# A two-layer graph network on one core: another buffer for the first score row, another place for half of the first mask's loads, and two copies and two comparisons of the last part moved to VectorE

## The chip, the cores and the metric

The kernel runs on one core of a Trainium2 chip. The metric is the device time of one execution in microseconds (us); before the change the median of three runs is 2143.52 us (2142.39 to 2146.54). The core has a matrix engine (TensorE, PE in the profile), VectorE (DVE), ScalarE (ACT), GpSimd (POOL) and SyncE (SP). SP and POOL issue DMA transfers here, each in the order of its own instruction stream.

## The reference, cut to what matters

```python
# 3327 nodes, 1024 features, adj 3327 x 3327 (about 1 % non-zero)
# layer 0
h = maximum(layernorm(x), 0);  x = x + quantised(adj @ quantised(relu(quantised(h) @ quantised(weight))))
# layer 1: 8 heads of 64
h = maximum(layernorm(x), 0)
Wh = einsum('nf,hfd->hnd', h, W)
e_src, e_dst = (Wh * a1).sum(-1), (Wh * a2).sum(-1)
e = where(adj > 0, leaky_relu(e_src[:, :, None] + e_dst[:, None, :], 0.2), -9e15)
h = elu(einsum('hnm,hmd->hnd', softmax(e), Wh))
enc = h.transpose(1, 0, 2).reshape(n, 512)
out = relu(enc @ W1.T + b1); out = relu(out @ W2.T + b2); out = relu(out @ W3.T + b3)
x = x + out @ W4.T + b4
```

## The kernel before, in words

Nodes are padded to 26 tiles of 128. The work has four stages, one after the other on TensorE.

**Stage 1** (to about 127 us) forms the quantised product of the first layer, `s_int`, one tile of 128 nodes at a time.

**Stage 2** (the loop at L709, to about 922 us) multiplies the adjacency by `s_int`. For each output tile t, column t of the adjacency comes from memory in four pieces (`PARTS`, L48: source tiles 0-6, 7-12, 13-19, 20-25), each into an `at` buffer (L186). ScalarE rounds it to `hi` (L190), VectorE forms `lo = at - hi` (L194), and TensorE multiplies both with `s_int` (L723). VectorE also writes a mask of non-zeros, which POOL stores to memory (`mask_d`, L201). Then ScalarE empties the sum into `y` (L738), VectorE adds x, which POOL stores (L741), and normalises it (L149). `transposed_by_dma` (L607) has ScalarE split `y` into 16-bit halves (`yh`, L616, two casts) and SP issue two transposing DMAs (`yht`, L618); ScalarE joins the halves again to `ht` (L622, two copies). `heads` (L645) multiplies `ht` by the weights of all heads (`whm`, L652, 16 passes), forms the scores of source and destination, their exponentials (`powers`: L672 and two at L692) and the features of the tile, which POOL stores (`feat_d`, L703). The product `whm` of tile t stands on TensorE ahead of the last piece of tile t+1. For tiles 24 and 25 there is no such cover: TensorE runs the adjacency product of tile 25, then `whm` of tile 24, then attention work in between. Tile 25 is transposed on TensorE itself in two groups of four (`tp`, L638) with one shared PSUM buffer; ScalarE copies each group out (L642).

**Stage 3**, attention (the loop at L954), is a list of 32 parts: 8 heads times 4 subsets of the output tiles (`SUBS`, 7, 6, 7 and 6 tiles). A part goes through 13 pairs of source tiles in seven groups (`GROUPS`, L49: pairs 0-1, 2-3, 4-5, 6, 7-8, 9-10, 11-12). `select` makes the 0/1 choice of a pair: `over` says where the score is positive, by two ScalarE instructions (L845) or, for the pairs in `BY_VECTOR`, two VectorE instructions (L839); two VectorE instructions combine it with the mask to `sel` (L854, L855). `over` has two buffers, `sel` six. `sums` multiplies `sel` with the features (`acc`, L874). `select` runs two groups ahead of `sums`. The score row of a part (`srow`, one row of `src_d` copied to all partitions, L809) has two pools with one buffer each, `srow1` for odd parts and `srow0` for even ones; a pool that is opened earlier gets the lower address. These pools lie in space that `at`, `hi` and `lo` used in stage 2, so their first use waits for the last reader of what lay there.

At the turn from stage 2 to stage 3 the order on each engine is set by `queue_behind` (an instruction stands behind another on its queue) and `tc.issue_after`. L930-L944 issue the first loads: the mask of part 0 in two halves (source tiles 0-12 and 13-25, seven transfers each) on POOL; on SP the first score row, the two transposing DMAs of tile 24 behind it (L932), the x rows of tile 25, the features of head 0 in three pieces (tiles 0-6, 7-19, 20-23), the second score row, then the other masks. `pin` keeps the order of stage 3 on each engine as written.

**Stage 4** is a network of four dense layers over groups of four tiles. Its first two layers for the first group are woven into the last part of stage 3: `join` (L1024) makes 32-bit features from two 16-bit halves by four ScalarE copies (k = 0 to 3), and `layer` (L1029) is a generator that yields after each matmul, with one PSUM buffer and a ScalarE relu after k = 3 (L1043). In the last part the loop takes (0, 0, 3, 3, 2, 2, 2) steps of it ahead of the sums of groups 0 to 6 (L1069-L1073), so that k = 3 of the first output block and k = 0, 1 of the second stand between groups 2 and 3. ScalarE's stream there holds, in order: the four copies of `join`, the four `over` of pairs 7 and 8, the cast `eh` (L920) of the previous part's result, the four `over` of pairs 9 and 10, the relu.

Of the kernel before, what the change touches and what calls it, by code (L numbers as in the profile page):

```python
# [24 lines left out]
T = (N + P - 1) // P  # L25
NP = T * P
TH = T // 2
# [39 lines left out]
def two_layer_kernel(  # L67
# [23 lines left out]
    nc = tc.nc  # L91
# [62 lines left out]
    def queue_behind(ins, other):  # L154

        tc.add_manual_dep(
            ins.ins,
            other.ins.name,
            mybir.DependencyInfo(mybir.DependencyClass.NoSync, mybir.DependencyReason.DATA),
            reason="queue_behind",  # L160
        )

    def halves_of_words(words):

        return words.bitcast(U16).rearrange("p (n two) -> p two n", two=2)
# [7 lines left out]
    with tc.tile_pool(name="at", bufs=2, reuse_waits="tile") as atp:  # L173
# [42 lines left out]
        with tc.tile_pool(name="s1", bufs=2, reuse_waits="tile") as s1, tc.tile_pool(  # L216
            name="s1_mm", bufs=3, space=PSUM, reuse_waits="tile"
# [8 lines left out]
            def pin(ins):  # L226
                tc.keep_in_program_order(ins)
# [336 lines left out]
            for t in range(8, T):  # L564
                if t == T - 2:
                    part = next(columns)
                pair = t // 2 + 2
# [25 lines left out]
        with tc.tile_pool(name="wh", bufs=1, reuse_waits="tile") as whp, tc.tile_pool(  # L593
            name="s2", bufs=2, reuse_waits="tile"
        ) as s2, tc.tile_pool(name="mm", bufs=2, space=PSUM, reuse_waits="tile") as mm_ps, tc.tile_pool(
            name="s2_wh", bufs=2, space=PSUM, reuse_waits="tile"
        ) as wh_ps, tc.tile_pool(name="s2_sp", bufs=1, space=PSUM, reuse_waits="tile") as sp_ps, tc.tile_pool(
            name="s2_last", bufs=1, space=PSUM, reuse_waits="tile"
# [32 lines left out]
            def transposed_by_tensor(y):  # L631

                ht = s2.tile([P, KF, P], F32, name="ht", bufs=1)
                ends, copies = [], []
                for g in range(KF // 4):
                    tp = last_ps.tile([P, 4, P], F32, tag="last", name="tp2")
                    turns = [
                        nc.tensor.transpose(tp[:, q, :], y[:, (4 * g + q) * P : (4 * g + q + 1) * P], ident)  # L638
                        for q in range(4)
                    ]  # L640
                    ends.append((turns[0], turns[-1]))
                    copies.append(nc.scalar.copy(ht[:, 4 * g : 4 * g + 4, :], tp))  # L642
                return ht, ends, copies
# [65 lines left out]
            for t in range(T):  # L709
                xt = s2.tile([P, F], F32, name="xt2")  # L710
# [49 lines left out]
            of_k, products, _, powers, _, taken = heads(*before, own=f_even)  # L760
            queue_behind(products[0], lacking)
            queue_behind(taken, lacking)
            ht, turns, copies = transposed_by_tensor(y)
            queue_behind(copies[0], taken)
            queue_behind(powers[0], copies[-1])
            last_of_k, *_ = heads(T - 1, ht, r, own=f_even)

    attends = [(h, si) for h in range(NH) for si in range(len(SUBS))]
    steps = [(i, g) for i in range(len(attends)) for g in range(len(GROUPS))]
    AHEAD = 2  # L770
    BY_VECTOR = (6,)

    with tc.tile_pool(name="over", bufs=2, reuse_waits="tile") as overp, tc.tile_pool(
        name="srow1", bufs=1, reuse_waits="tile"
    ) as srow1, tc.tile_pool(name="srow0", bufs=1, reuse_waits="tile") as srow0, tc.tile_pool(
        name="sel", bufs=6, reuse_waits="tile"
    ) as selp, tc.tile_pool(name="f1", bufs=1, reuse_waits="tile") as f1p, tc.tile_pool(
        name="s3", bufs=1, reuse_waits="tile"
    ) as s3, tc.tile_pool(
        name="s3_acc", bufs=7, space=PSUM, reuse_waits="tile"  # L780
# [11 lines left out]
        def load_features(h, js):  # L792
            r = slice(js[0], js[-1] + 1)
            return nc.sync.dma_start(
                (f_odd if h % 2 else f_even)[:, r], feat_d[r, h].rearrange("t p c -> p t c")
            )

        def load_mask(si, js=slice(0, T), queue=nc.sync):
            for b, t in enumerate(SUBS[si]):
                ins = queue.dma_start(masks[si][:, b, js], mask_d[t][:, js])  # L800
            return ins
# [3 lines left out]
        def load_src(i):  # L805
            h, si = attends[i]
            nb = len(SUBS[si])
            srows[i] = (srow1 if i % 2 else srow0).tile([P, 7 * P], F32, tag="srow", name="srow")[:, : nb * P]
            return nc.sync.dma_start(srows[i], src_d[si][h].partition_broadcast(P))  # L809
# [17 lines left out]
        def select(n):  # L827
            ends = {}
            i, g = steps[n]
            h, si = attends[i]  # L830
            nb = len(SUBS[si])
            mask = masks[si].bitcast(U32)
            for pair in GROUPS[g]:
                over = overp.tile([P, 2, 7 * P], U8, tag="over", name="over")[:, :, : nb * P]
                for q in range(2):
                    j = 2 * pair + q
                    if pair in BY_VECTOR:
                        pin(
                            nc.vector.tensor_scalar(  # L839
                                over[:, q], srows[i], ndst[:, j, h : h + 1], 255.0, ALU.is_gt, ALU.mult  # L840
                            )
                        )
                    else:
                        ends["scalar"] = pin(
                            nc.scalar.activation(  # L845
                                over[:, q], srows[i], AF.Relu, bias=large_dst[:, j, h : h + 1], scale=BIG
                            )
                        )
                        ends.setdefault("first", ends["scalar"])
                sel = selp.tile([P, 2, 7, 2, P], U8, tag="sel", name="sel")  # L850
                up, dn = (sel[:, q, :nb].bitcast(U32) for q in range(2))
                of_pair = mask[:, :, 2 * pair : 2 * pair + 2]
                over = over.bitcast(U32).rearrange("p q (b i) -> p b q i", b=nb)
                pin(nc.vector.tensor_tensor(up, over, of_pair, ALU.bitwise_and))  # L854
                ends["vector"] = pin(nc.vector.tensor_tensor(dn, up, of_pair, ALU.bitwise_xor))  # L855
                chosen[i, pair] = sel.bitcast(F8)
            return ends
# [69 lines left out]
                )  # L927
            yield

        for js in (slice(0, TH), slice(TH, T)):  # L930
            load_mask(0, js, nc.gpsimd)
        queue_behind(planes[0], load_src(0))  # L932
        with tc.issue_after(turned.ins):
            ins = load_features(0, range(7))
        with tc.issue_after(ins.ins):
            load_features(0, range(7, 20))
            load_features(0, range(20, T - 2))
            load_src(1)
            load_mask(1)
            load_mask(2)  # L940
            ins = load_mask(3)
        with tc.issue_after(ins.ins):
            load_features(1, range(T - 2))
            load_features(1, range(T - 2, T))  # L944
        ends = select(0)
        queue_behind(joins[0], ends["scalar"])
        queue_behind(joins[1], joins[0])
        queue_behind(emptied, joins[1])
        queue_behind(resumed, ends["vector"])
        select(1)  # L950
        turn = [(of_k[-1], turns[0][0]), (turns[-1][1], last_of_k[0]), (last_of_k[-1], None)]
        closed = None
        first_group = iter(())
        for n, (i, g) in enumerate(steps):  # L954
            if n + AHEAD < len(steps):
                ends = select(n + AHEAD)
                if n == 0:
                    queue_behind(ends["first"], taken)
# [6 lines left out]
            if (i, g) == (len(attends) - 1, 0):  # L965
# [4 lines left out]
                def nodes(name):  # L970
                    n = large(mlp, name, [P, WORDS])
                    return (
                        n[:, : 4 * EMB].bitcast(U16).rearrange("p (q r) -> p q r", q=2),
                        n[:, 4 * EMB : 4 * (EMB + F)].rearrange("p (q e) -> p q e", q=4),
                    )

                weights = large(mlp, "weights", [P, WORDS])
                enc_x1 = [nodes("nodes0")]
# [5 lines left out]
                h1_0, h2_0, enct0 = (  # L984
                    rest[:, F + 16 + 512 * at : F + 16 + 512 * (at + n)].rearrange("p (m c) -> p m c", c=512)
                    for at, n in ((0, D1 // P), (D1 // P, D2 // P), ((D1 + D2) // P, EMB // P))
                )
# [8 lines left out]
                def by_feature(enc, cols):  # L996

                    k = EMB // P
                    return enc[:, :, : k * cols].rearrange("p q (k c) -> p q k c", k=k)
# [21 lines left out]
                nc.sync.dma_start(bb4, b4.partition_broadcast(P))  # L1021
                load_encoded(1, range(4, 8))

                def join(xt, enc):  # L1024

                    for k in range(EMB // P):
                        pin(nc.scalar.copy(halves_of_words(xt[:, k]), by_feature(enc, 512)[:, :, k]))  # L1027

                def layer(yt, xt, wt, bt):  # L1029
                    for m in range(yt.shape[1]):  # L1030
# [37 lines left out]
                first_group = early_layers()  # L1068
            if i == len(attends) - 1:  # L1069
                if g == 1:  # L1070
                    join(enct0, enc_x1[0][0])
                for _ in range((0, 0, 3, 3, 2, 2, 2)[g]):
                    next(first_group)  # L1073
            first, last = sums(n)
# [9 lines left out]
            if (i, g) == (len(attends) - 1, 5):  # L1084
                weight_sums()
                join(joined_1, enc_x1[1][0])
# [5 lines left out]
    with tc.tile_pool(name="s4", bufs=2, reuse_waits="tile") as s4, tc.tile_pool(  # L1092
        name="s4_ps", bufs=4, space=PSUM, reuse_waits="tile"
# [172 lines left out]
```

## Time and profile before

| what | value |
|---|---|
| median of three runs | 2143.52 us (2142.39 to 2146.54) |
| the profiled execution | 2143.69 us |
| its span, first to last instruction | 2141.8 us |
| mean granted TensorE clock | 0.996 |
| busy: PE, DVE, ACT, POOL | 2099.7 (98%), 1392.0 (65%), 1346.9 (63%), 163.6 us (8%) |
| the chain that ended last | PE 94%, DVE 2%, DMA 2%, ACT 2% |
| HBM read, written | 141.21 MB, 66.02 MB |

All instants in the text are us from the start of the span, so 1.9 us of the profiled time lie around it. Busy time says how long instructions of an engine were in work. The chain of waits is followed back from the last instruction to whatever released each one. A row of the timeline gives start, length, engine, line, operation, tiles and count, and in brackets the idle time before it with its releaser; SPq rows are issues of DMAs, not the transfers. A row of the stretches gives the busy time of each engine, the granted TensorE clock as a share of full speed, the share of the 16 DMA engines in work (it can pass 1) and GB/s.

### The profile page before, as it was taken

How to read it: one execution, taken by the hardware profiler on the slowest of the kernel's cores; microseconds unless marked ns; L12 is line 12 of the kernel's file. 1: busy time of each engine (PE TensorE's matmuls, PEld its weight loads, DVE VectorE, ACT ScalarE, POOL GpSimd, SP SyncE). 2: the span in 40 equal slices, each digit the busy share in tenths (PEclk: the TensorE clock that was granted, in tenths of full speed). 3: DMA queues.
4: the chain of work that ended last, by engine and by line, in shares of the span. 5: the costliest groups of instructions: out<-in, count | busy, mean ns of one | idle time of the engine just before them, and what ended most of it. 6: DMA issues, size and time to landing. Idle time of an engine off the chain costs nothing.

```text
span 2141.8 us, 36615 instructions
## 1 busy us (share of the span) xinstructions
PE 2099.7 (98%) x15099; PEld 1690.6 (79%) x15109; DVE 1392.0 (65%) x2564; ACT 1346.9 (63%) x1752; POOL 163.6 (8%) x257
## 2 busy tenths in 40 slices
PE   5999999999999999999999999999999999999999
PEld 2467777777777777679999999999999999844444
DVE  8845556555655565477777777777777777545446
ACT  6734454545444544478888888888888888742321
POOL 2300000000100000300000000000000000000000
PEclk9999999999999999999999999999999999999999
DMA  6654544455445444791202012120202104443322
GB/s 221 171 167 137 161 149 138 144 166 146 139 142 169 153 130 139 182 312 26 74 17 72 25 36 63 26 67 21 74 26 74 26 17 133 108 108 127 107 89 74
DMA packets 183527, 233.21 MB, mean 109 GB/s; under 512 B 103924, under 2 KB 131268, under 8 KB 183360
## 3 DMA queue, kind: packets, MB, share of 16 engines
q1 hardware_dynamic: 167676, 175.42, 27.2%
q0 software_dynamic: 15616, 55.39, 8.4%
q8 instruction: 118, 1.93, 0.4%
q14 instruction: 49, 0.40, 0.1%
q10 hardware_dynamic: 68, 0.06, 0.0%
HBM read 141.21 MB, written 66.02 MB: 97 GB/s over the span
## 4 chain that ended last, share of the span: by engine, by line
PE 94%; DVE 2%; DMA 2%; ACT 2%; issue 0%; SPq 0%; POOL 0%; DVEq 0%; ACTq 0%; POOLq 0%
PE acc L874 42%; PE mm L723 28%; PE whm L652 8%; PE o L1176 7%; PE h_ps L1108 5%; PE mm L342 3%; DMA yht<-yh 1%; ACT over L845 1%; DMA xqt<-xq 0%; DVE stats L255 0%; DMA w<-in_w 0%; PE h_ps L1034 0%; ACT xb L314 0%; DVE w_stats L385 0%; ACT rest L1027 0%
## 5 line engine op out<-in xcount | busy, mean ns | idle before, releaser
L874 PEld LDWEIGHTS <-sel 128*128 128x128 fp8e4 x10816 | 932.3, 98 | 4.7 <-issue 3.1
L845 ACT ACTIVATE over<-srow,large_dst 128x896 uint8<-128x896 f32 (+1 forms) x768 | 686.1, 975 | 36.4 <-DVE sel L854 30.1
L874 PE MATMUL acc<-f_odd,sel 128*128 128x195 bf16 x5408 | 467.6, 247 | 0.0
L874 PE MATMUL acc<-f_even,sel 128*128 128x195 bf16 x5408 | 467.0, 247 | 0.0
L723 PE MATMUL mm<-s_int,hi 128*128 128x512 f32 x1352 | 426.3, 396 | 0.0
L723 PE MATMUL mm<-s_int,lo 128*128 128x512 f32 x1352 | 416.5, 389 | 0.0
L854 DVE TENSOR_TENSOR sel<-over,mask 128x448 uint32<-128x448 uint32 (+1 forms) x416 | 243.8, 586 | 223.9 <-ACT over L845 121.2
L723 PEld LDWEIGHTS mm<-s_int,hi 128*128 128x128 f32 x1352 | 254.0, 188 | 62.5 <-issue 11.5
L723 PEld LDWEIGHTS mm<-s_int,lo 128*128 128x128 f32 x1352 | 253.7, 188 | 52.8
L855 DVE TENSOR_TENSOR sel<-sel,mask 128x448 uint32<-128x448 uint32 (+1 forms) x416 | 245.9, 591 | 14.2
L652 PE MATMUL whm<-whead,ht 128*128 128x512 f32 x416 | 185.8, 600 | 6.4 <-ACT ht L622 6.4
L190 ACT CAST hi<-at 128x896 fp32r<-128x896 f32 x104 | 92.4, 888 | 152.4 <-PE mm L723 73.4
L195 DVE TENSOR_SCALAR mk<-at 128x896 uint8<-128x896 f32 (+1 forms) x104 | 59.4, 590 | 169.2 <-DMA at<-in_adj_t 169.0
L652 PEld LDWEIGHTS whm<-whead,ht 128*128 128x128 f32 x416 | 79.8, 192 | 97.6 <-issue 88.5
L194 DVE TENSOR_TENSOR lo<-at,hi 128x896 fp32r<-128x896 f32 x104 | 106.1, 1020 | 68.2 <-ACT hi L190 68.1
L922 POOL DMA_DIRECT2D enc_d<-eh x64 | 57.5, 903 | 864.3 <-ACT eh L920 837.6
L907 ACT ACTIVATE ht<-su,rs 128x64 f32<-128x64 f32 x208 | 53.1, 335 | 107.6 <-DVE rs L903 107.6
L893 DVE TENSOR_REDUCE su<-acc 128x130 f32<-128x390 f32 x208 | 115.6, 556 | 7.9 <-PE acc L874 7.9
L1118 ACT ACTIVATE h<-h_ps,rest 128x512 f32<-128x512 f32 (+1 forms) x52 | 33.7, 654 | 118.7 <-PE h_ps L1108 118.7
L342 PE MATMUL mm<-w_int,xqt 128*128 128x512 bf16 x406 | 93.9, 385 | 6.9 <-DVE w_int L473 4.5
L659 ACT ACTIVATE wht<-whm,lnr 128x512 f32<-128x512 f32 x26 | 17.9, 687 | 124.9 <-PE whm L652 114.9
L622 ACT COPY ht<-yht 128x1024 uint16<-128x1024 uint16 x50 | 67.4, 1355 | 32.4 <-DMA yht<-yh 32.3
(189 smaller groups left out, 1687.5 us busy)
## 6 DMA issues: line engine op xcount, KB each, us to landing
at<-in_adj_t SPq DMA_DIRECT2D x52, 448.0 KB, 4.6
feat_d<-fw POOLq DMA_DIRECT2D x26, 780.0 KB, 6.0
at<-in_adj_t SPq DMA_DIRECT2D x52, 384.0 KB, 4.0
x_d<-xt POOLq DMA_DIRECT2D x26, 512.0 KB, 2.9
nodes<-x_d SPq DMA_DIRECT2D x26, 512.0 KB, 5.2
xt<-in_x SPq DMA_DIRECT2D x25, 512.0 KB, 3.9
out<-yo SPq DMA_DIRECT2D x50, 256.0 KB, 2.2
xs<-in_x SPq DMA_DIRECT2D x24, 512.0 KB, 4.2
```

What stands on the lines that cost most here:

```text
L190: ins = nc.scalar.copy(hi, at)
L194: nc.vector.tensor_tensor(lo, at, hi.bitcast(F32), ALU.subtract)
L342: nc.tensor.matmul(mms[t][:, r], xqts[t][:, k, :], w_int[:, k, r], start=(k == 0), stop=(k == KF - 1))
L652: ins = nc.tensor.matmul(whm, ht[:, k, :], whead[:, k, :], start=(k == 0), stop=(k == KF - 1))
L723: nc.tensor.matmul(mm[:, c * 512 : (c + 1) * 512], which[:, q, :], s_int[j][:, c * 512 : (c + 1) * 512], start=(j == 0 and which is hi), s ...
L845: nc.scalar.activation(over[:, q], srows[i], AF.Relu, bias=large_dst[:, j, h : h + 1], scale=BIG)
L854: pin(nc.vector.tensor_tensor(up, over, of_pair, ALU.bitwise_and))
L855: ends["vector"] = pin(nc.vector.tensor_tensor(dn, up, of_pair, ALU.bitwise_xor))
L874: ins = nc.tensor.matmul(accs[i, b][:, r], chosen[i, pair][:, s, b, q], f[:, j, r], start=(j == 0 and s == 0), stop=(j == T - 1 and s == 1),)
L893: nc.vector.tensor_reduce(su[:, b], accs.pop((i, b)).rearrange("p (q s c) -> p q c s", q=2, s=3), AX.X, ALU.add)
L1108: ins = nc.tensor.matmul(pss[m][:, :cols], wt[:, k, m * P : (m + 1) * P], xt[:, k, :cols], start=(k == 0), stop=(k == k_n - 1),)
L1176: nc.tensor.matmul(ps, st[:, k, q // 2], mv[:, k], start=(k == 0), stop=(k == 1))
```

## The change

- All three `powers` of tile 24 stand behind the second copy of the transposed tile 25 on ScalarE, not only the first of them.
- The pools `srow0` and `srow1` are opened in the other order, so their addresses swap.
- Of the first mask only the half of source tiles 0-12 stays on POOL. The half of tiles 13-25 goes to SP, behind the first piece of the features, which now has eight tiles; the second piece has twelve.
- In the last part, pair 8's `over` is made by VectorE as well as pair 6's.
- In the last part's `join`, copies k = 1 and k = 3 are made by VectorE. The later `join` of the second group keeps four ScalarE copies.

```diff
-            queue_behind(powers[0], copies[-1])
+            for power in powers:
+                queue_behind(power, copies[-1])
...
-    BY_VECTOR = (6,)
+    BY_VECTOR = (6,), (6, 8)
...
-        name="srow1", bufs=1, reuse_waits="tile"
-    ) as srow1, tc.tile_pool(name="srow0", bufs=1, reuse_waits="tile") as srow0, tc.tile_pool(
+        name="srow0", bufs=1, reuse_waits="tile"
+    ) as srow0, tc.tile_pool(name="srow1", bufs=1, reuse_waits="tile") as srow1, tc.tile_pool(
...
-                    if pair in BY_VECTOR:
+                    if pair in BY_VECTOR[i == len(attends) - 1]:
...
-        for js in (slice(0, TH), slice(TH, T)):
-            load_mask(0, js, nc.gpsimd)
+        load_mask(0, slice(0, TH), nc.gpsimd)
         queue_behind(planes[0], load_src(0))
         with tc.issue_after(turned.ins):
-            ins = load_features(0, range(7))
+            ins = load_features(0, range(8))
         with tc.issue_after(ins.ins):
-            load_features(0, range(7, 20))
+            ins = load_mask(0, slice(TH, T))
+        with tc.issue_after(ins.ins):
+            load_features(0, range(8, 20))
             load_features(0, range(20, T - 2))
...
-                def join(xt, enc):
+                def join(xt, enc, by_vector=()):

                     for k in range(EMB // P):
-                        pin(nc.scalar.copy(halves_of_words(xt[:, k]), by_feature(enc, 512)[:, :, k]))
+                        copy = nc.vector.tensor_copy if k in by_vector else nc.scalar.copy
+                        pin(copy(halves_of_words(xt[:, k]), by_feature(enc, 512)[:, :, k]))
...
-                    join(enct0, enc_x1[0][0])
+                    join(enct0, enc_x1[0][0], (1, 3))
```

## The prediction

> **What bounds the kernel now.** I read the page first: PE is busy 98% and carries 94% of the chain, so only time in which TensorE idles or runs slowly can be won. The list of TensorE's waits then says where it idles. After the start-up (waits before 127 us, which the change doesn't touch) three are left:
>
> ```profile
> PE whm L652 <- ACT ht L622: 6.4, 1, 6.4
> PE h_ps L1034 <- ACT rest L1043: 2.9, 1, 2.9
> PE tp L638 <- ACT ht L642: 2.2, 1, 2.2
> ```
>
> These are 11.5 us, two at the turn to attention and one in the last part. The chain of waits at the turn shows what stands behind the first:
>
> ```profile
> 895.20 0.97 DVE lo L194
> 896.17 0.02 issue
> 896.19 0.33 SPq L809
> 896.52 0.05 issue
> 896.57 13.94 DMA yht<-yh
> 910.50 0.02 issue
> 910.53 1.34 ACT ht L622
> 911.86 0.04 issue
> 911.91 10.07 PE whm L652 x16
> ```
>
> The score row's issue (L809) waits for the last `lo`, because its buffer lies where that `lo` reads; the transposes stand behind it on SP although their first input was cast at 891.99 and the second at 894.43 (timeline, `yh` L616). They land at 910.5, TensorE has been out of work since 905.5. The last row is 10.07 us for 16 passes that take 6.87 in every other tile. The stretches say why (after ":" length, then busy times, granted clock, DMA share, GB/s):
>
> ```profile
> 905.50:907.30 1.80, 0.03 (x1) 0.00 (x0) 1.25 (x2) 0.00 (x0) 0.00 (x0) 1.00 1.00 256
> 907.30:911.90 4.60, 0.00 (x0) 0.00 (x0) 0.00 (x0) 1.37 (x2) 0.00 (x0) 0.53 1.17 207
> 911.90:917.60 5.70, 5.69 (x7) 2.53 (x8) 3.46 (x5) 5.70 (x6) 0.55 (x1) 0.50 1.10 309
> 1856.07:1859.49 3.42, 3.42 (x6) 1.32 (x7) 1.67 (x3) 3.25 (x4) 0.00 (x0) 0.56 0.00 0
> ```
>
> About 2 us into the idle time the clock falls to half and stays there for 5.7 us of work. The fourth row is the same after the idle time in the last part.
>
> **Part 1, the first score row.** Built, the new order lets the row wait for the `lo` of source tiles 7-12, which ends at 883.42, not 896.16. It is issued by then, while the DMA share is 0.05, and lands by about 889 (5.6 us from issue before). Nothing else changes in its cost. The `over` that read it move up to 895.2 on ScalarE, behind the last `hi`, and end at 899.0 (3.85 us), so that the joins of `ht` find ScalarE free.
>
> The transposes then go at 892.05 and 894.5. How long do they take? Clean, tile 23's took 3.1 us each. At the turn it was 13.9, with the score row in front on the same queue and POOL's second mask half beside it. Now the first half lies beside them (POOL issues it from 889.02 to 893.14, behind 780 KB of `feat_d`): of its 1.49 MB, about 1.25 MB is left at 893.5. So contention doesn't vanish. Bounds: from below, clean, both landed by 898; from above, as slow as before, 894.5 + 13.9 = 908.4. Before, the packets of the two (256 B each, 2048 in all) ran from 900.2 to 910, that is 10 us beside 1.1 MB of mask. I take this, as the nearest row: 893 to 903, landed at 903.5 and 904.5. A copy of `ht` takes 1.34, so the first half is there at 904.9 and the second at 906.3; TensorE needs the first at 905.5 and the second 3.4 later. That hides the transposes, with 0.6 us to spare. I deduct 0.5 for the chance that it is a little late.
>
> Gain: 6.4 of idle time and, since without it the clock has no cause to fall, 10.07 - 6.87 = 3.2; less 0.5: 9.1 us.
>
> What the rule says: the Trainium skill (TensorE: Matmul & The Clock Gate, Part 1: The HAM clock gate) has the clock go to half after an idle window of about 3.4 us and return after about as long a busy one. For this wait it gives 3.4 at half speed, 1.7 us lost; the row says 3.2, and I use the row. For the last part it speaks against the change, see there.
>
> **Part 2, half of the mask on SP.** It takes seven issues from POOL (896.03 to 899.7) and puts them behind the features' first piece on SP. A rule against it: the Trainium skill (DMA: Bandwidth & Descriptors, Issuing engines are not separate DMA queues) says that all issuers share the same 16 engines, so another issuer saves bytes nowhere. The trace agrees (share about 1 from 888 on), and by that rule alone the part is worth nothing. But the order changes: 1.49 MB no longer run beside the transposes, and that is already in part 1. What comes later? The x rows: issued at 897 to 899 rather than 902.9, moved right behind the transposes (1.6 us before) by about 906, needed at 907.6. Features: eight tiles rather than seven; their 780 B packets ran at some 425 per us, so 2.4 us, and a landing 1.3 later, at about 909.5; `acc` needs them when `whm` ends, 905.5 + 6.87 = 912.4. The mask half: at the 331 to 410 GB/s of the rows around it, 3.6 to 4.5 us, so 914 to 915. VectorE needs it for pair 6 at 918 at the earliest, and TensorE needs pair 6 at 935. The features 8-19 (1170 KB, 3.6 us) land at 919, needed at 930. The later masks slip by some 4 us, but start about as much earlier; mask 1 landed well ahead of its use at 953.67. SP's waiting issues hold only loads. Cost: nothing, by this cover; each us beyond it would cost a us.
>
> **Part 3, the exponentials.** Before, ScalarE had the table load (1.28) and two small exponentials between the fourth `over` and the copy that `tp` waits for. Now the stream is five `over`, copy, one `over`, copy, table load. Counted from the end of `whm`: cast 0.7, five `over` at 0.95, so the copy can start at 5.4; `tp`'s first four end at 4.83 + 0.6 = 5.43. The copy takes 0.5, and the gap is about 0.55 instead of 2.25: gain 1.7. Behind it wait the features of tile 24 (`ft`, `fw`), needed by TensorE some 30 us later, and the load for head 1, later still. VectorE takes pairs 6 and 7 before `ft`, which keeps it busy meanwhile.
>
> After that TensorE runs without a gap to the last part, as now; `over` and `sel` follow it through their buffers (pair 10's `sel` at 946.98 waited for `acc`), so the earlier start is kept.
>
> **Part 4, the last part.** The rows of TensorE and of ScalarE:
>
> ```profile
> 1852.09 1.05 PE L1034 MATMUL h_ps<-rest,weights 128*128 128x512 f32 x2
> 1856.07 3.42 PE L1034 MATMUL h_ps<-rest,weights 128*128 128x512 f32 x4 [2.94 <-ACT rest L1043]
> 1861.64 1.90 PE L1034 MATMUL h_ps<-rest,weights 128*128 128x512 f32 x4
> ...
> 1843.12 4.92 ACT L1027 COPY rest<-nodes 128x1024 uint16<-128x1024 uint16 x4
> 1852.04 3.41 ACT L845 ACTIVATE over<-srow,large_dst 128x768 uint8<-128x768 f32 x4
> 1855.35 0.67 ACT L1043 ACTIVATE rest<-h_ps,rest 128x512 f32<-128x512 f32 x1
> ```
>
> The matmul before the relu ends at 1853.1; the relu waits for the `over` ahead of it until 1855.4. Taken from ScalarE: two copies at 1.23 and two `over` at 0.85, 4.2 us. So its `over` of pairs 9 and 10 end at 1851.3 at the earliest; the second pair's buffer comes free when VectorE has used pair 8, 1850.5, so 1852.3. Either way the relu starts when the matmul ends and TensorE waits some 0.75 (0.67 and two hand-overs): 2.9 - 0.75 = 2.2 gained. VectorE gets two copies, which the trace doesn't show there: 0.75 by its one-input 1024-element row (L149), 1.24 by its two-input ones (L1066); I take 1.2. They fall into its 4.6 us of idle time before 1849.69: copies to 1846.9, `ht` to 1847.5, pair 7 to 1848.7, pair 8's `over` (1.14) to 1849.9. k = 1 is copied by 1845.8, when TensorE asks at 1846.2; even at twice the price it would cost below 1 us.
>
> The clock: 2.94 us of idle time are less than the rule's window of 3.4, so by the rule nothing slows and the part is worth 2.2. The row has clock 0.56, 3.42 us for four passes where 1.74 is usual in the chain, and 24 `acc` in 2.31 rather than 4.13 / 2 = 2.07. By the row another 1.9, together 4.1. I take the row; a wait of 0.75 should leave the clock up.
>
> **The sum.** 9.1 + 1.7 + 4.1 = 14.9. From the profiled 2143.69: 2128.8 us, 1.9 of it around the span. The median before is 0.17 lower, nothing beside the error.
>
> **The rivals.**
> - *The transposes land late.* In favour: the DMA share is about 1 from 888 on, and rows of 902 to 905 moved only 70 to 100 GB/s; against it, POOL's second half is gone. At the upper bound, 908.4, TensorE idles about 4 us and the clock falls: part 1 keeps 6.4 - 4 = 2.4, all 3.2 of slow work stays: 2.4 + 1.7 + 4.1 = 8.2, so 2135.5.
> - *The last part gains nothing*, since VectorE, with 3.5 us more, makes ScalarE's `over` wait for buffers: 9.1 + 1.7 = 10.8, so 2132.9. Against: its 4.6 us of idle time.
> - *Both*: 3.9, so 2139.8, no difference that can be told.
> - *Slower: the mask half arrives too late on SP.* Place: VectorE stands before pair 6's `sel` (L854), with `ft`, pairs 7 and 8 behind it, and TensorE behind them. It begins to cost when the half lands after 934, and eats the whole gain from 949; at 955 the time is 2150. In favour: SP's 19 mask issues took 20.5 us, with waits for one another (9.8 us). Against: seven of these are 7.6 us, from 909 to 917.
> - *The swap doesn't free the row*: excluded by the built order, which names the earlier `lo`.
>
> **How the numbers follow.** All parts as summed 0.65 (2126.5 to 2131.5: from a gain of all 11.5 us of idle time and 5.1 of slow clock to transposes 2 us late), late transposes 0.19, no gain at the end 0.07, both 0.05, slower 0.04. The range 2126.5 to 2136.0 holds the first three. What a measurement can tell from no change is about 0.2%, 4.3 us: faster 0.91, same 0.05, slower 0.04.
>
> **What would show it.** Right: the score row issued near 883.5; transposes issued at 892 and 894.5 and landed before 905; `whm` of tile 24 in about 6.9 us from 905.6; clock 1.00 throughout; `acc` of pairs 4 and 5 starting near 931 (941.86 before); the gap before `tp` near 0.5, and before the relu's matmul near 0.75. Wrong: `whm` waiting on `ht` over 2 us with the clock at half, a wait of `acc` for features, or VectorE idle before pair 6's `sel` on a DMA.

## The result, and the profile after

The kernel after takes 2133.90 us (median of 5 runs, 2132.73 to 2134.62) against 2143.90 (5 runs, 2142.39 to 2146.54) for the kernel before, run beside it: ratio 0.9951, 95% interval 0.9936 to 0.9966. It is faster by 10.0 us; 14.9 was forecast. The profiled execution took 2132.73 us (2143.69 before) with a span of 2131.0, which is 10.8 less than before. Source lines of the kernel after are shifted by 1 to 3 (L845 is L846, L874 is L875, L1034 is L1037).

TensorE's list of waits after the start-up (total, times, longest), to be set beside the three of before:

```profile
PE tp L638 <- ACT ht L642: 2.1, 1, 2.1
PE h_ps L1037 <- ACT rest L1046: 0.8, 1, 0.8
PE acc L875 <- DVE su L894: 0.5, 1, 0.5
```

The wait of `whm` (6.4) is gone, and that in the last part is down to 0.8. The wait of `tp` has hardly moved, and a small one for a closing sum (`su`) is new. The timeline of SP at the turn (start, length of the issue), then that of ScalarE, with the two copies that join what the transposes bring:

```profile
883.63 0.33 SPq L810 DMA_DIRECT2D srow<-src_d  x1
892.19 6.72 SPq L618 DMA_TRANSPOSE yht<-yh  x2
```

```profile
902.49 2.56 ACT L622 COPY ht<-yht 128x1024 uint16<-128x1024 uint16 x2 [3.39 <-DMA yht<-yh]
```

The row goes at 883.6, the transposes from 892.2, and ScalarE, which had waited 3.39 us for them, starts the first join at 902.5. So 10.3 us from issue to landing, without a row in front and without the second mask half beside them, is still far from the 3.1 of tile 23. TensorE's timeline shows what this is worth at the turn and in the last part:

```profile
905.56 7.03 PE L652 MATMUL whm<-whead,ht 128*128 128x512 f32 x16
...
919.98 0.66 PE L638 MATMUL tp<-ident,y 128*128 128x128 f32 x4 [2.12 <-ACT ht L642]
...
1846.40 1.98 PE L1037 MATMUL h_ps<-rest,weights 128*128 128x512 f32 x4 [0.78 <-ACT rest L1046]
```

`whm` starts when the adjacency product ends, at full clock (7.03 rather than 10.07). The relu's matmuls take 1.98 rather than 3.42.

Laying TensorE's records of the two traces side by side, one by one, shows where the time went (gains of the span; a loss has a minus):

| stretch | forecast | measured |
|---|---|---|
| start-up (its end lies anywhere from 125.2 to 127.5 us in the traces of this document) | 0 | -0.2 |
| `whm` of tile 24: its end at 912.59 rather than 921.96, start-up put back | 9.1 | 9.6 |
| gap before `tp`: 2.12 rather than 2.25 | 1.7 | 0.1 |
| pairs and closings of the first two parts, 954 to 987 | 0 | -2.0 |
| last part | 4.1 | 3.8 |
| rest | 0 | -0.5 |
| sum | 14.9 | 10.8 |

### The profile page after: what moved, and what is told of

Same layout as the page of the kernel before. It is cut to its first block, busy times and chain, and to the rows that moved or that the text cites. A ratio compares the mean times of both kernels' runs of the same rounds, so it can differ in the third digit from the quotient of the medians.

```text
span 2131.0 us, 36616 instructions
## 1 busy us (share of the span) xinstructions
PE 2096.3 (98%) x15099; PEld 1689.4 (79%) x15109; DVE 1395.4 (65%) x2568; ACT 1343.1 (63%) x1748; POOL 160.7 (8%) x250
## 4 chain that ended last, share of the span: by engine, by line
PE 92%; ACT 2%; DVE 2%; DMA 2%; issue 2%; SPq 0%; POOL 0%; DVEq 0%; POOLq 0%; ACTq 0%
PE acc L875 41%; PE mm L723 28%; PE whm L652 8%; PE o L1179 7%; PE h_ps L1111 5%; PE mm L342 3%; ACT over L846 1%; DMA feat_d<-fw 1%; PE h_ps L1037 1%; DMA xqt<-xq 0%; DMA w<-in_w 0%; DVE stats L255 0%; ACT xb L314 0%; DMA xt<-in_x 0%; DVE w_stats L385 0%
## 5 line engine op out<-in xcount | busy, mean ns | idle before, releaser
L875 PEld LDWEIGHTS <-sel 128*128 128x128 fp8e4 x10816 | 932.1, 97 | 5.9 <-issue 4.6
L846 ACT ACTIVATE over<-srow,large_dst 128x896 uint8<-128x896 f32 (+1 forms) x766 | 684.4, 975 | 30.0 <-DVE sel L855 30.0
L875 PE MATMUL acc<-f_even,sel 128*128 128x195 bf16 x5408 | 468.2, 248 | 0.6 <-DVE su L894 0.5
L875 PE MATMUL acc<-f_odd,sel 128*128 128x195 bf16 x5408 | 467.4, 247 | 0.0
```

Of the source, the lines that this page charges most:

```text
L846: nc.scalar.activation(over[:, q], srows[i], AF.Relu, bias=large_dst[:, j, h : h + 1], scale=BIG)
L875: ins = nc.tensor.matmul(accs[i, b][:, r], chosen[i, pair][:, s, b, q], f[:, j, r], start=(j == 0 and s == 0), stop=(j == T - 1 and s == 1),)
```

## Theories and experiments

**C (contention).** What made the transposes late was the second mask half on POOL beside them, more than the row in front; part 2 then carries the gain that the forecast booked under the row. Rival (S in the expectations): the row carries it. **F (feature store).** The 2.0 us come from `fw`, which has one buffer: ScalarE's first write of tile 25's `fw` waits for tile 24's store. Rivals: the two engines merely have too much to do, or (M) the store is slow whatever the exponentials do. **G (`over` in front of the copy).** The gap before `tp` stays because the fifth `over`, ahead of ScalarE's copy, waits for VectorE. In the first four runs (with the kernel before at 2144.42 in the same series) one part at a time is done or undone.

**The swap of the row's buffer alone**

```diff
-        name="srow1", bufs=1, reuse_waits="tile"
-    ) as srow1, tc.tile_pool(name="srow0", bufs=1, reuse_waits="tile") as srow0, tc.tile_pool(
+        name="srow0", bufs=1, reuse_waits="tile"
+    ) as srow0, tc.tile_pool(name="srow1", bufs=1, reuse_waits="tile") as srow1, tc.tile_pool(
```

> Only the pools of the score rows are swapped; the mask halves, the exponentials and the last part are as before. Theory C (the second mask half beside the transposes matters): POOL issues that half at 896, the two transposes share the DMA engines with 1.49 MB more, the first lands at 906 to 909, TensorE idles 2 to 5 us before whm of tile 24, the clock falls again, and 2 to 5 us of the 9.6 won by the changed kernel there are left: 2139 to 2142 us. Rival S (the score row in front was all): transposes land by 904, TensorE doesn't idle, 2134 us.

Measured: 2142.71 us (13 runs), ratio 0.9993 [0.9984, 1.0001]. The group of tile `yht` in its trace (the two joins with their first and last start, then ScalarE's idle time before them, then who waited for them):

```profile
L622 ACT COPY ht<-yht x2: 1327/1340/1354, 904.8 to 913.7; 128x1024 uint16<-128x1024 uint16 x2
...
  DMA yht<-yh: 12.7, 2
...
  PE whm L652: 5.2, 1
```

The row was out of the way at 884.2 and the transposes were issued at 892.7 and 895.2. The first half was joined at 904.8, but the second only at 913.7: POOL's second mask half, issued from 897.1 to 901.1, ran beside it. The wait only moved from the first half to the second. This is for theory C, though the time fell by less than its 2 to 5 us: the interval holds 1, so no gain of the swap alone is shown.

**The change with both mask halves on POOL (part 2 undone)**

```diff
-        load_mask(0, slice(0, TH), nc.gpsimd)
+        for js in (slice(0, TH), slice(TH, T)):
+            load_mask(0, js, nc.gpsimd)
...
-            ins = load_features(0, range(8))
-        with tc.issue_after(ins.ins):
-            ins = load_mask(0, slice(TH, T))
-        with tc.issue_after(ins.ins):
-            load_features(0, range(8, 20))
+            ins = load_features(0, range(7))
+        with tc.issue_after(ins.ins):
+            load_features(0, range(7, 20))
```

> The changed kernel with both mask halves on POOL and the feature pieces of seven and thirteen tiles as before. Theory C: transposes land 3 to 6 us later than in the changed kernel (902.5), whm of tile 24 starts at 908 to 910 with the clock at half, and the time is 4 to 7 us above the changed kernel: 2137 to 2140 us. Rival S: within 1 us of the changed kernel, 2133 us.

Measured: 2139.11 us (21 runs), ratio 0.9977 [0.9970, 0.9983]. From TensorE's list of waits:

```profile
PE whm L652 <- ACT ht L622: 3.2, 1, 3.2
PE tp L638 <- ACT ht L642: 3.0, 1, 3.0
```

After both waits the clock is down (0.57 and 0.60 over the next 4 us). The joins start at 902.7 and 910.7, so again the second half is late. Set beside the 0.9951 of the kernel after, taking part 2 away costs 0.26%, 5.6 us, and the two intervals don't touch.

**The change with the old exponentials (part 3 undone)**

```diff
-            for power in powers:
-                queue_behind(power, copies[-1])
+            queue_behind(powers[0], copies[-1])
```

> The changed kernel with only the first exponential of tile 24 behind the copies, as before. Theory F (moving the exponentials delays the store of tile 24's features, whose buffer tile 25 waits for; ScalarE stood 5.3 us there, and TensorE lost about 1.9 us at the end of parts 0 and 1): store issued 3 us or more earlier than 930.5, ScalarE's wait for it under 2 us, the gap before tp again about 2.2, and 1 to 2 us less than the changed kernel: 2131 to 2132 us. Rival M (the store is slow because the mask loads now run beside it, whatever the exponentials do): the wait stays at 4 us or more, time as the changed kernel, 2133 us.

Measured: 2132.11 us (5 runs), ratio 0.9944 [0.9932, 0.9956]: no slower than with part 3, the intervals overlap. In the trace the gap before `tp` is 2.5 with the clock at 0.62 behind it, which costs 0.4 and 1.6 us against the kernel after. But tile 24's store is issued at 928.05 rather than 930.53 (2.5 us earlier, where theory F had asked for 3), tile 25's `fw` no longer waits for it, and by 987 TensorE has won the same 2.0 back. Part 3 thus took away work of 1.6 us ahead of ScalarE's copy (1.28 for the table, 0.3 for the exponentials), and what that won was lost again at the closings. This is for F; the size needs a run with F's cause removed.

**The last part alone (part 4 on the kernel before)**

```diff
-    BY_VECTOR = (6,)
+    BY_VECTOR = (6,), (6, 8)
...
-                    join(enct0, enc_x1[0][0])
+                    join(enct0, enc_x1[0][0], (1, 3))
```

> The kernel before with only the last part changed (pair 8's comparisons and copies k = 1 and 3 on VectorE). By the rows of the profile (2.2 us of idle time and 1.9 us of half clock): TensorE's wait for the relu 0.8, clock 1.00 after it, 3.8 us less than before, 2140 us. Rival (the clock's fall has another cause and stays): 2.2 us less, 2141.6 us.

Measured: 2139.39 us (11 runs), ratio 0.9978 [0.9969, 0.9987], that is 4.7 us (2.8 to 6.6); the gap before the relu's matmuls is 0.8. The interval holds the 4.1 of the forecast; a gain without the clock's share (2.2) lies outside it. Record by record the last part alone gives 3.8; the rest of this trace's lead lies in the start-up and at the turn.

The next four kernels ran in a second series, with the kernel before at 2143.33.

**Two buffers of `fw`**

```diff
-                    srct = s2.tile([P, P], F32, name="srct")
+                    srct = s2.tile([P, EMB], F32, tag="prod", name="srct", bufs=1)[:, :P]
...
-                fw = s2.tile([P, NH, 2, 3, HC], BF16, name="fw", bufs=1)
+                fw = s2.tile([P, NH, 2, 3, HC], BF16, name="fw", bufs=2)
```

> The kernel after, with a second buffer for `fw` (the room comes from placing `srct` in the buffer of `prod`); the order on every engine is unchanged. Theory F: in the kernel after, ScalarE's first write of `fw` of tile 25 waited 5.34 us for tile 24's feature store, which runs beside the mask loads, and this is what puts the streams of ScalarE and VectorE behind and costs the 1.9 us that TensorE lost between 954 and 986. Then the wait is gone or under 1.5 us and for `ft`, TensorE waits less for the closings `su`, and the time falls by 1.5 to 1.9 us, to about 2132 (ratio to before near 0.9943). Rival: the write is only one of several things that the two engines queue for (the work behind it is as long as before), the wait turns into waits elsewhere, and the time stays within 0.5 us of the kernel after (ratio 0.9949 to 0.9953).

The room comes from `srct`, which now uses the buffer of `prod`; the order on every engine is unchanged.

Measured: 2131.78 us (2130.62 to 2132.89), ratio 0.9943 [0.9929, 0.9956]. ScalarE's timeline, first of the kernel after, then of this one:

```profile
936.38 0.32 ACT L692 ACTIVATE ft<-dst 128x8 f32<-128x8 f32 x2 [1.24 <-DVE dst L667]
942.03 1.07 ACT L697 CAST fw<-ft 128x1040 bf16<-128x1040 f32 x1 [5.34 <-DMA feat_d<-fw]
```

```profile
938.27 1.07 ACT L697 CAST fw<-ft 128x1040 bf16<-128x1040 f32 x1 [1.26 <-DVE ft L693]
```

The wait of 5.34 us for a DMA becomes one of 1.26 for VectorE. Record by record, with the difference at start-up (0.3) taken out, TensorE wins 0.7 us over the kernel after at 954.7 and 2.0 by 987, which is the whole loss, and the wait for `su` is gone. The ratios differ by 0.0008, 1.7 us, within their intervals, so the trace decides here. Theory F holds: the closings of 954 and 987 were late because ScalarE and VectorE had stood behind that store.

**The copy ahead of the fifth `over`**

```diff
                 if n == 0:
                     queue_behind(ends["first"], taken)
+                if n == 2:
+                    queue_behind(ends["first"], copies[0])
```

> The kernel after, with ScalarE's copy of the first group of `tp` put ahead of the fifth `over` of pair 2's stretch. Theory G: the gap of 2.12 us before `tp` stayed because the fifth `over` waits 1.13 us for VectorE's `sel` (only two `over` buffers) with the copy behind it. Then the gap falls to about 0.6, TensorE comes 1.5 us earlier to the pairs behind, and, as far as the wait for the feature store doesn't swallow it, the time falls by up to 1.5 us: 2132.4, ratio near 0.9944. Rival: the gap goes, but the wait of `fw` for the store and the closings set the pace behind it, and the time stays within 0.5 us of the kernel after.

Measured: 2130.99 us (2130.32 to 2131.91), ratio 0.9939 [0.9927, 0.9952]; the gap is 0.68, and TensorE is 1.3 us ahead of the kernel after there and 1.7 at 954. That the store would swallow part of it was feared and did not come: ScalarE still waits 5.0 us for it, but TensorE only 0.2 for `su`. The interval overlaps with that of the kernel after, so here too the trace decides. Theory G holds.

**Both**

```diff
+                if n == 2:
+                    queue_behind(ends["first"], copies[0])
...
-                fw = s2.tile([P, NH, 2, 3, HC], BF16, name="fw", bufs=1)
+                fw = s2.tile([P, NH, 2, 3, HC], BF16, name="fw", bufs=2)
```

(`srct` is placed as in the run with two `fw`.)

> Both edits: two buffers of `fw`, and the copy of `tp` ahead of the fifth `over`. If both theories hold and the gains add, 3.2 to 3.5 us under the kernel after: about 2130.5, ratio near 0.9937. If the two are one and the same slack (the streams of ScalarE and VectorE set the pace in either case), no more than the better of the two alone: 2132 to 2132.5.

Measured: 2129.33 us (2128.07 to 2129.65), ratio 0.9930 [0.9917, 0.9942]. Its range touches neither of the two single ones. Record by record TensorE is 4.7 us ahead of the kernel after by 987: 1.2 from the start-up, 1.5 at the gap before `tp` and 2.0 at the closings; so the two gains add. The timeline of ScalarE, first of the kernel after, then of this one:

```profile
913.46 3.83 ACT L846 ACTIVATE over<-srow,large_dst 128x896 uint8<-128x896 f32 x4
918.42 1.04 ACT L846 ACTIVATE over<-srow,large_dst 128x896 uint8<-128x896 f32 x1 [1.13 <-DVE sel L855]
919.37 0.56 ACT L642 COPY ht<-tp 128x512 f32<-128x512 f32 x1
```

```profile
912.24 3.83 ACT L846 ACTIVATE over<-srow,large_dst 128x896 uint8<-128x896 f32 x4
916.68 0.59 ACT L642 COPY ht<-tp 128x512 f32<-128x512 f32 x1 [0.61 <-PE tp L638]
917.22 1.04 ACT L846 ACTIVATE over<-srow,large_dst 128x896 uint8<-128x896 f32 x1
```

In the kernel after, the fifth `over` waits 1.13 us for a buffer that VectorE's `sel` holds, and the copy behind it starts 2.1 us after the fourth `over` ended; here it waits only for its own input. This version is faster than the kernel before. It was not run in one series with the kernel after: the two ratios are 0.9951 and 0.9930, their intervals overlap by 0.0006, and the step between these two kernels rests on the traces, where 3.4 us are won behind the start-up.

**The change without the swap**

```diff
-        name="srow0", bufs=1, reuse_waits="tile"
-    ) as srow0, tc.tile_pool(name="srow1", bufs=1, reuse_waits="tile") as srow1, tc.tile_pool(
+        name="srow1", bufs=1, reuse_waits="tile"
+    ) as srow1, tc.tile_pool(name="srow0", bufs=1, reuse_waits="tile") as srow0, tc.tile_pool(
```

> The kernel after with the score rows' buffers in the old order, so that the first row again waits for the last `lo` (issued near 896.2 rather than 884) and the transposes stand behind it (896.5 rather than 892.2 and 894.6). The half of the mask stays on SP. Theory W: in the kernel after the transposes' first packets left only at 896.2, when the first mask half on POOL had nearly run out, so that the earlier issue bought little; with the second half off POOL they run at once from 897 on and land near 904 to 906, `whm` begins its wait-free run 1 to 3 us later than in the kernel after, and the time is 1 to 4 us above it: 2135 to 2138, ratio 0.996 to 0.997. Rival: the order of the row and the transposes is what matters, and without it part 1's 9.6 us are lost: 2143, ratio 0.999 or above.

Measured: 2134.36 us (2133.34 to 2134.99), ratio 0.9954 [0.9942, 0.9967], against 0.9951 with the swap: 0.0003, well inside the intervals. `whm` waits 0.5 us and starts 0.8 later than in the kernel after, and the gap before `tp` is 2.7 with the clock at 0.57 behind it (1.6 us of this trace's loss). ScalarE's timeline:

```profile
901.26 3.85 ACT L846 ACTIVATE over<-srow,large_dst 128x896 uint8<-128x896 f32 x4 [5.78 <-DMA srow<-src_d]
905.01 2.53 ACT L622 COPY ht<-yht 128x1024 uint16<-128x1024 uint16 x2
```

The transposes were issued at 896.9 and 898.2, over 3.6 us later than in the kernel after, and the trace has the first landed 5.2 us after issue, at 902.1: no later than the 902.5 with the swap. The packets say why. In the kernel after the first packets of the transposes (256 B) ran at 896.2, 4 us after issue, and until 902 they got some 70 to 400 per us beside the last of POOL's first mask half; without the swap they began at 899, when POOL's packets had run out, and reached 1071 per us. The earlier issue only waited (the 16 DMA engines were full meanwhile: share 1.03 from 892 to 896). The transposes landed before the 904 to 906 that theory W named, and the loss by the medians is below its 1 to 4 us. What the swap does win is on ScalarE, as the forecast said of the joins: without it the four `over` run when the late row lands, from 901.3 rather than 895.3, and the joins behind them start at 905.0 rather than 902.5.

The last four ran in a third series, with the kernel before at 2145.03.

**The mask half on SP alone (part 2 on the kernel before)**

```diff
-        for js in (slice(0, TH), slice(TH, T)):
-            load_mask(0, js, nc.gpsimd)
+        load_mask(0, slice(0, TH), nc.gpsimd)
...
-            ins = load_features(0, range(7))
+            ins = load_features(0, range(8))
...
-            load_features(0, range(7, 20))
+            ins = load_mask(0, slice(TH, T))
+        with tc.issue_after(ins.ins):
+            load_features(0, range(8, 20))
```

> The kernel before with part 2 alone: the second mask half on SP behind the first eight tiles of features, everything else as before (row after the last `lo`, old exponentials, last part on ScalarE). Theory C: the mask half beside the transposes was what delayed them; they land near 905 without the row being moved, the wait of `whm` falls from 6.4 to about 0.5 us and the clock stays up there; part 4's 3.75 us and part 1's last 1 us are missing, and the gap before `tp` is 2.3 to 2.7 with or without the clock: a gain of 5 to 7.5 us, 2136 to 2138.5, ratio 0.9965 to 0.9977. Rival: it takes both (the row moved and the mask half moved), and part 2 alone gives under 2 us: ratio over 0.999.

Measured: 2137.19 us (2135.97 to 2138.65), ratio 0.9965 [0.9952, 0.9977]. The group of `yht`:

```profile
L618 SPq DMA_TRANSPOSE yht<-yh x2: 1237/2296/3355, 897.2 to 898.4; - x2
...
  PE whm L652: 1.1, 1
...
DMA to landing us min/median/max: 5.7/5.7/5.7
```

The row is still in front of the transposes and they still go at 897, yet they land at 902.9 rather than 910.5, `whm` waits 1.1 rather than 6.4, and 0.35% is won, clear of noise, where the swap alone won 0.07%, which is not. Record by record, this edit gives 8.2 of the 9.6 us that the kernel after wins by the end of tile 24's `whm`. Theory C is shown from both sides: with the half elsewhere the order hardly matters, with the half in place neither order helps. One thing stays open. The half was moved off POOL's queue and behind the transposes in one edit; the same half issued later on POOL was not run, so that it is the time and not the queue is argued from the packets.

**The last part with the copies only**

```diff
-    BY_VECTOR = (6,), (6, 8)
+    BY_VECTOR = (6,), (6,)
```

> The kernel after with pair 8 of the last part back on ScalarE; of part 4 only the two join copies stay on VectorE. Theory: in the kernel after ScalarE stood idle for 0.8 (waiting for `sel`) and 0.85 us ahead of the relu, which together is about what two `over` of pair 8 cost it (1.7), so the relu still starts within 0.4 us of its matmul's end, the gap of TensorE stays near 0.8 to 1.2, the clock stays up, and the time is that of the kernel after within 0.5 us (ratio 0.995). Rival: both pieces are needed, and with either gone the gap is over 2.5 us, the clock falls, and 3.75 us are lost: ratio 0.9969.

**The last part with pair 8 only**

```diff
-                    join(enct0, enc_x1[0][0], (1, 3))
+                    join(enct0, enc_x1[0][0])
```

> The kernel after with all four join copies on ScalarE; of part 4 only pair 8 stays on VectorE. ScalarE gets 2.45 us back against some 1.65 us of idle time ahead of the relu. Theory: the relu comes 0.8 to 0.9 us late, the gap is about 1.7, the clock stays up (it stayed up at gaps of 2.12 to 2.27 and fell at 2.5 and more), and the time is 0.9 us above the kernel after: ratio 0.9955. Rival: as for the run before, a gap over 2.5 with the clock down, ratio 0.9969.

Measured: 2132.61 us (2131.55 to 2133.73), 0.9943 [0.9929, 0.9957], for the copies; 2136.90 (2136.09 to 2137.97), 0.9964 [0.9952, 0.9977], for pair 8. TensorE's timeline in the first and in the second, then the stretch of the second behind this gap:

```profile
1846.99 1.98 PE L1037 MATMUL h_ps<-rest,weights 128*128 128x512 f32 x4 [0.78 <-ACT rest L1046]
```

```profile
1848.75 1.94 PE L1037 MATMUL h_ps<-rest,weights 128*128 128x512 f32 x3 [2.19 <-ACT rest L1046]
```

```profile
1848.80:1852.80 4.00, 4.00 (x13) 2.18 (x14) 1.62 (x3) 3.20 (x4) 0.00 (x0) 0.62 0.01 2
```

The two copies do the whole of part 4: with pair 8 back on ScalarE the gap is the same 0.78, since ScalarE's stream had idle time for it. For pair 8 alone the middle was expected (gap 1.7, clock up) and missed: the gap is 2.19, because the 0.8 us for which ScalarE waits for a buffer did not shrink when its stream came later, and the clock fell behind it. Between the two kernels lie 4.3 us by the medians. The traces put 3.1 of them in the last part (1.4 of gap, 1.7 of slow clock) and 1.0 at the turn, where the clock of the second fell behind the same gap of 2.12 us; the last section says when it does.

**Both additions, old exponentials** (on the kernel with two `fw` and the early copy)

```diff
-            for power in powers:
-                queue_behind(power, copies[-1])
+            queue_behind(powers[0], copies[-1])
```

> Two buffers of `fw` and the copy of `tp` ahead of the fifth `over`, as in the best run so far, but with part 3 undone: the table load (1.28 us) and the exponentials on `ft` (0.31) stand ahead of the copy on ScalarE. Theory: with the fifth `over` out of the way part 3 is worth what it meant to be: undone, the copy starts about 1.0 us later (1.6 less the 0.6 us for which ScalarE waited there), the gap before `tp` is about 1.7 with the clock up, and the time is 1 us above that run: ratio 0.9935. Rival: the features that come earlier make up for it, and the time is the same or lower: ratio 0.9925 to 0.993.

Measured: 2130.50 us (2129.82 to 2131.34), ratio 0.9933 [0.9921, 0.9946]. The gap before `tp` is 1.57 rather than 0.68, as expected; the times differ in the same direction, but the intervals overlap. So with the fifth `over` out of the way part 3 takes 0.9 us off the gap. The medians don't show that this reaches the time; record by record, the 0.9 stay to the end of the span.

## Why the prediction held, and where its steps failed

The time lies in the forecast's range because the two largest terms came true and the range was 9.5 us wide; of the 14.9 us forecast, 10.0 came.

**The turn.** The instants of part 1 came true: row at 883.63 (883.5 forecast), transposes at 892.19 and 894.65 (892.05 and 894.5), first join at 902.5 (903.5), `whm` in 7.03 us (6.87) from 905.56, clock 1.00. Of 9.6 us, 9.1 had been forecast. The joint gain was right, but its reason was split wrongly. The text treats the row as the thing that holds the transposes and says of part 2 that its effect "is already in part 1"; alone, the row is worth 0.07%, not clear of noise, and the mask half 0.35%. That the landing fell within 1 us of the forecast is in part luck: the packets were to run from 893 to 903, and ran from 896.2 to 903. With the row still in front the transposes land 5.7 us after their issue once the half is gone, where they had taken 13.94. What the text says on the rule that another issuer saves no bytes stands: the 1.49 MB were still moved, and what was won is that they moved later than the transposes. None of the feared costs of part 2 came: the half ran from 907 to 911 (914 to 915 forecast), and no `acc` waited for features.

**Part 3 failed in the step "five `over` at 0.95, so the copy can start at 5.4".** It took ScalarE's work without its waits. `over` has two buffers, so each `over` beyond them waits for `sel`: the fifth waited 1.13 us, and the copy came 6.8 us after the end of `whm`. Before, this wait lay hidden behind the table load and the exponentials (1.6 us); taking them out exposed it. Gain 0.1 rather than 1.7.

**"So the earlier start is kept" failed.** The text cleared tile 24's features because TensorE needs them "some 30 us later". The reader that mattered was another: tile 25's first write of `fw`, which has one buffer. With the turn shorter, tile 25's exponentials came 9.1 us earlier (936.38 rather than 945.51). Tile 24's store was issued only 5.8 earlier (930.53 rather than 936.31) and took 11.4 us beside the mask loads rather than 9.3, so that it landed only 3.6 earlier. The margin was gone: 5.3 us of wait on ScalarE, 2.0 lost on TensorE.

**Part 4** held with 3.8 us for 4.1, and so did the choice of the row over the rule: the gain without the clock's share was measured out of range. In all three traces with this gap of 2.9 to 3.0 us (before, swap alone, mask half on SP alone) the clock fell behind it. The copies on VectorE cost 0.68 us each rather than 1.2; the timeline of VectorE:

```profile
1836.99 1.36 DVE L1030 COPY rest<-nodes 128x1024 uint16<-128x1024 uint16 x2
```

It was a mis-sized term without effect on the sum, as these copies lie in idle time.

The three missed terms (1.6 of the gap, 2.0 of the closings, 0.3 of the last part) and the 0.7 of start-up and rest, less 0.5 won more at `whm`, are the 4.1 between forecast and profile.

**"Clock 1.00 throughout"** came true by luck at the gap before `tp`: it was still 2.12 us long, and behind the same gap the clock of the run with pair 8 only fell.

## What to carry to other kernels

When a transfer is late, ask which bytes share its engines between issue and landing before asking what stands in front of it on its queue: moving 1.49 MB behind the transposes alone won 0.35%, issuing them 4 us earlier alone nothing clear of noise (0.07%). When a stage is made shorter, look through every single buffer behind it whose release is a DMA, since its landing does not move up with the engines. And work out when an instruction can start from its engine's waits, not from the lengths of the rows ahead of it: work that is taken out may only have been hiding a wait.

## Not expected of the hardware

- *The clock after short idle times.* The gaps of TensorE before `tp` in these traces, with the granted clock in the 4 us behind: 2.12 (kernel after) 1.00, 2.12 (pair 8 only) 0.66, 2.25 (before) 1.00, 2.27 (last part alone) 1.00, 2.51 (old exponentials) 0.62, 2.70 (without the swap) 0.57, 3.01 (halves on POOL) 0.60, 3.07 (mask half on SP alone) 1.00, 3.33 (swap alone) 0.61. Between 2.1 and 3.1 us the clock falls or doesn't, so the gap's length alone does not decide. The clock's own records in the traces show what does. After the start-up every stretch at half speed lasts 3.41, 6.82 or 10.24 us (but for the one that runs past the end of the span), and within one trace all changes of the clock lie on one grid of 3.413 us: in the kernel before the clock changes at 907.57, and again 3, 278 and 279 steps later (917.81, 1856.48, 1859.89). Where the clock fell nowhere in between, the change at the end of the span gives the grid. Here are two steps of the kernel after, then two of the run with pair 8 only, around the same gap (after ":" the length, then PE's busy time; the granted clock is third from the end):

```profile
914.79:918.20 3.41, 3.07 (x35) 2.83 (x32) 3.38 (x8) 2.50 (x3) 0.00 (x0) 1.00 1.09 357
918.20:921.62 3.42, 1.64 (x18) 1.63 (x19) 3.26 (x7) 3.19 (x5) 0.00 (x0) 1.00 1.01 388
```

```profile
917.95:921.36 3.41, 1.29 (x14) 1.22 (x14) 3.25 (x7) 2.80 (x4) 0.00 (x0) 1.00 1.02 383
921.36:924.77 3.41, 3.41 (x24) 3.17 (x22) 2.85 (x5) 3.38 (x7) 0.00 (x0) 0.50 1.04 408
```

  A step's edge cuts the gap of the first into 0.34 and 1.78 us, and the clock stays up; the gap of the second lies in one step, and the clock falls at its end. So it is throughout these 14 traces, for all gaps over 0.3 us after the start-up: no step at full speed with up to 1.83 us of gap was followed by half speed, every one with 2.04 us or more was (13 of them), and no step lies between. The 3.07 us that kept the clock were cut into 1.41 and 1.66. Where the grid lies relative to the work differs from trace to trace. The Trainium skill (TensorE: Matmul & The Clock Gate, Part 1: The HAM clock gate) describes a free-running window of about 3.4 us. The grid agrees with that; but the window need not be idle throughout, since 2.04 us of it were enough here.
- *Transposes beside large packets.* The same two transposes landed 5.2 us after issue when POOL's packets (up to 4992 B) were nearly done, 10.3 beside the end of one mask half, and 13.9 with the second one following and the score row in front. In the kernel before, their 256 B packets ran at some 20 to 490 per us beside POOL's, in the kernel after at 70 to 400; alone, they reached 1071 (without the swap) and 1120 (mask half on SP alone).
